# A four-layer graph network: the placing of the edges and the masks of two groups are shared out anew among the engines

## The chip, the cores and the metric

The kernel runs on one core of a Trainium2 chip. The core has a TensorE (PE in the profile, with its weight loads as PEld), a VectorE (DVE), a ScalarE (ACT), a GpSimd (POOL) and a SyncE (SP), which only issues DMAs; ScalarE and GpSimd issue DMAs too (ACTq, POOLq). Each engine runs its own instructions in order and waits for others by semaphores. The metric is the device time of one execution in microseconds, the median over several.

## The reference, cut to what matters

A graph of 3125 nodes with 128 features and 100,000 edges, sorted by their destination, goes through four layers; each takes the layer norm and relu of x and adds its output to x.

```python
edge_index = jnp.stack([src, dst])
h = jnp.maximum(_layernorm(x, axis=-1), 0.0)
x = x + _L0_gnn_ref(h, edge_index, ...)                  # two attention layers of 4 heads
h = jnp.maximum(_layernorm(x, axis=-1), 0.0)
x = x + _L1_gnn_ref(h, edge_weight, weights, src, dst)   # three steps of a recurrence with the weighted adjacency
h = jnp.maximum(_layernorm(x, axis=-1), 0.0)
x = x + _L2_gnn_ref(h, src, dst, ...)                    # three rounds of mean over neighbours
h = jnp.maximum(_layernorm(x, axis=-1), 0.0)
x = x + _L3_gnn_ref(h, edge_index, edge_type_16, ...)    # a message of each edge, relu, mean by destination
```

One attention layer of `_L0_gnn_ref`, with a loop edge at each node:

```python
e = jax.nn.leaky_relu(al_src[src] + al_dst[dst], NEG_SLOPE)
m = jax.ops.segment_max(e, dst, num_segments=N)
w = jnp.exp(e - m[dst])
denom = jax.ops.segment_sum(w, dst, num_segments=N)
out = jax.ops.segment_sum(h[src] * (w / denom[dst])[:, :, None], dst, num_segments=N)
```

## The kernel before, in words

**Blocks and slots.** Nodes are cut into 25 blocks of 128. The adjacency is handled as 25 x 25 pairs of a destination block `db` and a source block `sb`. Each pair has `CAP[db]` slots of 128 lanes in a table in HBM (`self.table`, one row of 64 bytes for each lane). An edge's place is (base of its pair, in slots) times 128, plus its rank within the pair: the rank's upper part chooses the slot, its lower seven bits the lane.

**Placing the edges** (`place_edges`, from line 936). The edge arrays are loaded as 112 rows of 896 (line 955 the body, 956 the last row), after GpSimd has filled the ends of the tiles (953). dst, edge_weight and the shifted dst go by SP's queue, src and edge_type by ScalarE's. The load of x (`load_x`, lines 113 to 115, called in `graph_and_layer0`) is in SP's queue as well, and a fill of the table with -1 (`table<-none`, line 961, 10.9 MB). VectorE then takes blocks and parities out of the indices (968 to 981), counts how runs go on from row to row (989 to 998), and works in two halves of columns (`HALVES`: 512 and 384 of the 896): for each half the **block terms** `cap` and `base` as sums of steps over db (1037 to 1048), the ranks by 13 rounds of a masked running sum (1053 to 1056), the place out of rank, cap and base (1060 to 1081), then a transpose and the integer indices (1087, 1088). GpSimd **scatters** the edges by 782 indirect DMAs of 128 rows (1096), in the order `ORDER`: destination blocks from 5 up first, blocks 0 to 4 last. Each block needs a run of these scatters, `LOW[db]` to `ENDS[db]`. A **test** on VectorE (1107 to 1118) counts the edges below each block and notes in `self.bad` if those runs wouldn't do; if anything in `bad` is set at the end, a general version of the kernel runs.

**Building and attending** (`graph_and_layer0`). After the layer norm and the first projection (lines 1425, 1426 and on), the groups of destination blocks (5 to 8), (9 to 12), ... (21 to 24), (0 to 2), (3, 4) are taken in turn. `build_block` loads a block's slots (1167, one buffer), transposes the keys (1173), makes one-hot matrices on VectorE (1190, 1192) and multiplies them on TensorE (1204, 1207) into counts and weights, which ScalarE takes out (1211, 1212). For blocks below 6, ScalarE also copies rows (1177) and lanes (`wide_dl`, 1181). A **count check** on ScalarE (1217) sees whether any count is above 15. `attend` makes, for each head and each source block, a mask of the group's destinations and multiplies it on TensorE (1379). In the first attention VectorE makes each mask (1365, reading `ps_row` in PSUM and the counts). In the second attention, after all building, two of three masks are VectorE's and every third is ScalarE's and GpSimd's: sign and relu (1359, 1360), then the product with the counts (1362); ScalarE needs a copy of the row in SBUF for it (1483).

**Order.** The order of the instructions on each engine is not that of the code alone: the framework places an instruction whose operands are free where its engine has room (in the profile the fill of `rank`, line 1050, and of `beyond`, line 1113, stand at 1.1 and 1.95 us, ahead of the loads).

Layer 1 (from line 1488) streams the weights back from HBM, layer 2 (1622) multiplies by the counts in SBUF (1722) for groups of five blocks, layer 3 (1821) fetches messages.

Of the kernel before, what the change touches and what calls it, by code (L numbers as in the profile page):

```python
# [18 lines left out]
P = 128  # L19
# [21 lines left out]
GB = 5  # L41
# [23 lines left out]
BATCH = 8  # L65
SL, DL, WT, TYPE = 0, 1, 2, 5
# [834 lines left out]
class FastGnn(Gnn):  # L901
# [24 lines left out]
    def place_edges(self, placed):  # L926
# [9 lines left out]
        with ExitStack() as s:  # L936
# [20 lines left out]
            nc.gpsimd.memset(rec, 0.0)  # L957
# [40 lines left out]
            V.tensor_copy(carry, ps[:A, :n_pair])  # L998
# [14 lines left out]
            nc.scalar.copy(sb, sb_i)  # L1013
            d0, d1 = tile("d0"), tile("d1")
# [15 lines left out]
            t_cap, t_base, t_step, t_rank, t_r, t_hi, t_lane, t_level = (tile(m, dt) for m, dt in names)  # L1030
            idx = {}
            for i, (q0, n0) in enumerate(HALVES):
                lo, hi = q0 * P, (q0 + n0) * P
                cut = lambda t: t[:, lo:hi]

                cap, base, step, of_db = cut(t_cap), cut(t_base), cut(t_step), cut(db)
                V.tensor_scalar(cap, of_db, 24.0, 8.0, op0=OP.is_gt, op1=OP.mult)
                V.tensor_scalar(cap, cap, 1.0, None, op0=OP.add)
                V.tensor_scalar(base, of_db, float(N_SLOTS[-1]), None, op0=OP.mult)
                for d in range(NB - 1):  # L1040
                    for _ in range(CAP[d] - CAP[d + 1]):
                        V.scalar_tensor_tensor(cap, of_db, d + 0.5, cap, op0=OP.is_lt, op1=OP.add)
                    more = N_SLOTS[d] - N_SLOTS[d + 1]
                    if more:
# [22 lines left out]
                whole_of(hi_i, r_i, OP.arith_shift_right, 7)  # L1067
                whole_of(r_i, r_i, OP.bitwise_and, 127)
# [35 lines left out]
            left = t_level  # L1104
# [5 lines left out]
            upto = work.tile([P, NB], F32, name="upto")  # L1110
            V.tensor_copy(upto, ps[:, :NB])
            beyond = work.tile([P, 2, NB], F32, name="beyond")
            V.memset(beyond, 0.0)
# [21 lines left out]
    def open_build(self, s, counts):  # L1135
        nc, tc = self.nc, self.tc
        self.counts = counts.tile([P, NB, NP], FP8, name="counts8")
        self.weights = self.dram.tile([NB, P, NP], F32, name="weights")
        self.wide = self.dram.tile([2, sum(N_SLOTS[:WIDE]) * P], BF16, name="wide")
        one = self.b_one = s.enter_context(tc.tile_pool(name="build", bufs=1))  # L1140
        self.b_slots = s.enter_context(tc.tile_pool(name="build_s", bufs=1))
        self.b_hot = s.enter_context(tc.tile_pool(name="build_hot", bufs=2))
        self.b_out = s.enter_context(tc.tile_pool(name="build_out", bufs=3))
        self.b_ps = s.enter_context(tc.tile_pool(name="build_ps", bufs=2, space=PSUM))
        self.b_keys = s.enter_context(tc.tile_pool(name="build_keys", bufs=1, space=PSUM))
        self.lane16 = one.tile([P, P, 2], BF16, name="lane16")
        nc.vector.tensor_copy(self.lane16, bc(self.lane[:, :, None], [P, P, 2]))
        self.minus_most = one.tile([P, 1], F32, name="minus_most")
        nc.vector.memset(self.minus_most, -MOST)
        self.above = one.tile([P, NB], F32, name="above")  # L1150
        self.junk = one.tile([P, NB, P], FP8, name="junk")

    def build_block(self, db):
# [28 lines left out]
        for x0 in range(0, n_slots, BATCH):  # L1182
# [10 lines left out]
            for x in range(k):  # L1193
# [15 lines left out]
                if last and (j == 1 or sb == NB - 1):  # L1209
# [3 lines left out]
                    if sb % 4 == 3 or sb == NB - 1:  # L1213
# [3 lines left out]
        nc.scalar.activation(self.junk, self.counts[:, :, db * P : (db + 1) * P], AF.Relu, bias=self.minus_most,  # L1217
                             accum_out=self.above[:, db : db + 1], saturate=False)
# [115 lines left out]
    def attend(self, suffix, a, b, pools):  # L1334
# [4 lines left out]
        n = b - a  # L1339
        at, cols = slice(a, b), slice(a * P, b * P)  # L1340
# [3 lines left out]
        for q in range(n):  # L1344
            wide = u_tile()
            for sb in range(NB):
                nc.tensor.matmul(wide[:, : HEADS * 3 * F1], lhsT=self.counts[:, sb, (a + q) * P : (a + q + 1) * P],  # L1347
                                 rhs=parts[:, sb, :, :, F1:], start=(sb == 0), stop=(sb == NB - 1))
            V.tensor_reduce(u[:, q], wide[:, : HEADS * 3 * F1].rearrange("p (h s f) -> p h f s", h=HEADS, s=3),
                            axis=AX.X, op=OP.add)  # L1350
        sums = None
        for i in range(HEADS):
            row, own = row_of(lambda j: bc(self.sd[:, a + j, 1, i : i + 1], [P, P]), n)

            def mask(sb, row=row, own=own, i=i):

                if beside and sb % 3 == 2:
                    above = beside[0].tile([P, most * P], BF16, name="above0")[:, : n * P]
                    nc.scalar.activation(above, own, AF.Sign, bias=self.sd[:, sb, 0, i : i + 1])
                    nc.scalar.activation(above, above, AF.Relu)  # L1360
                    over = beside[1].tile([P, most * P], BF16, name="over")
                    nc.gpsimd.tensor_tensor(over[:, : n * P], above, self.counts[:, sb, cols], op=OP.mult)  # L1362
# [45 lines left out]
    def graph_and_layer0(self, counts, node):  # L1408
# [3 lines left out]
        with ExitStack() as s:  # L1412
            one = s.enter_context(tc.tile_pool(name="l0", bufs=1))
            self.open_attention(one)
            with ExitStack() as s2:
# [3 lines left out]
                super().load_x()  # L1419
# [10 lines left out]
            with ExitStack() as s2:  # L1430
# [196 lines left out]
    def layer2(self):  # L1627
        nc, tc = self.nc, self.tc
        last = 3 * D
        with ExitStack() as s:  # L1630
# [79 lines left out]
            for g in range(GN):  # L1710
# [3 lines left out]
                prepare(g, 0)  # L1714
            for i in range(3):
                n = last + (i == 0)
                ready = []
                for g in range(GN):
                    for db in range(g * GB, (g + 1) * GB):
# [10 lines left out]
                        nc.vector.scalar_tensor_tensor(own[:, db, :], t, inv, own[:, db, :], op0=OP.mult, op1=OP.add)  # L1730
                    finish(g, i)
# [3 lines left out]
                if i == 1:  # L1735
                    self.message_weights(one, ps_msg)
# [298 lines left out]
```

## Time and profile before

| what | us |
|---|---|
| median of 3 runs | 3201.25 (3200.83 to 3203.47) |
| the profiled execution | 3195.56 |
| its span, first to last instruction | 3193.8 |
| busy in it: PE, PEld | 2561.2, 1825.5 |
| busy in it: DVE, ACT, POOL | 2296.6, 917.4, 1445.2 |
| scatters (L1096) on POOL, 782 | 773.6 busy, 336.7 idle before them |
| masks on DVE (L1365), 1040 | 699.3 |
| masks' products on POOL (L1362), 160 | 211.3 |

The mean granted clock of TensorE was 0.959. By stage: edges and placing to about 175 us, first projection to 233, building and the first attention to about 1305, the second attention to 1725, layer 1 to 2200, layer 2 to 2640, layer 3 to the end.

How to read the lines: a timeline line has the start and the duration in us, the engine, the line of the code, the operation, output<-inputs, the shape, how many were merged, and in brackets how long the engine was idle before and what ended that. A line of the groups has the count after "x", then the busy time in us and the mean in ns of one, then the idle time before them with its releasers. "PEld" is a weight load, "SPq" an instruction on SP's DMA queue. The slices cut the span into 40 parts of 80 us; a digit is the busy share in tenths.

### The profile page before, as it was taken

What the parts mean: (1) busy time and instruction counts of PE and PEld (TensorE: products, weight loads), DVE (VectorE), ACT (ScalarE), POOL (GpSimd) and SP (SyncE); (2) the same over time, 40 slices, a digit from 0 to 9 for tenths busy, and PEclk for the clock granted to TensorE, in tenths of its full rate; (3) what the DMA queues carried; (4) which work ended last, traced back from release to release, by engine and by line L of the source; (5) the groups of instructions that cost most, each with busy time, mean ns of one, the idle gap of its engine ahead of it and who ended that gap; (6) DMA issues with size and microseconds to landing.
All of it is one profiled execution on the core that took longest, in us unless ns stands there. A gap on an engine that the chain in (4) does not pass through costs nothing. (4 is left out here: it accounts for less than half of the span.)

```text
span 3193.8 us, 52069 instructions
## 1 busy us (share of the span) xinstructions
PE 2561.2 (80%) x20788; PEld 1825.5 (57%) x20788; DVE 2296.6 (72%) x4015; ACT 917.4 (29%) x1785; POOL 1445.2 (45%) x1394
## 2 busy tenths in 40 slices
PE   0018787878787788798886999997999976989898
PEld 0017464646455655477675444445555546888897
DVE  7979999999989899899997010405455575666766
ACT  3035050505140212476665000002120212333333
POOL 1577777777777700055553000000120106777775
PEclk9979999999999999899999999998999997999999
DMA  6013130303131101000002878781000004444443
GB/s 187 14 18 98 25 98 20 98 20 101 31 94 28 51 32 62 1 2 1 1 1 80 298 272 302 273 301 45 1 1 1 5 18 138 130 139 133 128 131 85
DMA packets 127742, 276.54 MB, mean 87 GB/s; under 512 B 28645, under 2 KB 68468, under 8 KB 116532
## 3 DMA queue, kind: packets, MB, share of 16 engines
q1 hardware_dynamic: 62982, 198.30, 18.9%
q0 software_dynamic: 37856, 32.76, 4.8%
q10 hardware_dynamic: 26652, 42.05, 3.7%
q8 instruction: 165, 2.70, 0.4%
q14 instruction: 87, 0.71, 0.1%
HBM read 210.00 MB, written 63.02 MB: 85 GB/s over the span
## 5 line engine op out<-in xcount | busy, mean ns | idle before, releaser
L1096 POOL DMA_INDIRECT table<-rec,idx x782 | 773.6, 989 | 336.7 <-issue 237.4
L1365 DVE SCALAR_TENSOR_TENSOR over<-ps_row,minus,counts 128x512 bf16<-128x512 f32 (+3 forms) x1040 | 699.3, 748 | 15.9 <-ACT row L1483 12.0
L1379 PE MATMUL ps_acc<-parts,over 128*128 128x198 bf16 x5000 | 571.4, 251 | 134.1 <-POOL over L1362 34.7
L1379 PEld LDWEIGHTS <-over 128*128 128x128 bf16 x5000 | 391.8, 98 | 309.7 <-DVE over L1365 231.9
L1910 POOL DMA_INDIRECT m_far<-pre,src x401 | 397.8, 992 | 259.1 <-DVE skips L923 137.2
L1207 PE MATMUL ps_cw<-oh_w,oh_d 128*128 128x128 bf16 x4050 | 385.9, 224 | 56.7 <-DVE oh_w L1192 52.1
L1533 PE MATMUL ps_sum<-g,node 128*128 128x512 f32 (+1 forms) x1050 | 413.2, 552 | 12.9 <-DMA g<-weights 12.9
L1362 POOL TENSOR_TENSOR over<-above,counts 128x640 bf16<-128x640 bf16 x160 | 211.3, 1329 | 392.0 <-ACT above L1360 265.2
L1207 PEld LDWEIGHTS <-oh_d 128*128 128x128 bf16 x4050 | 303.8, 100 | 90.9 <-issue 68.7
L1204 PE MATMUL ps_cw<-oh_d,oh_s 128*128 128x128 bf16 x1350 | 299.0, 224 | 48.2 <-ACT w_out L1212 24.7
L1722 PE MATMUL ps_agg<-l_parts,counts 128*128 128x384 bf16 (+1 forms) x1875 | 317.3, 327 | 14.0 <-POOL l_parts L923 14.0
L1192 DVE TENSOR_TENSOR oh_w<-oh_s,keys 128x1024 bf16<-128x1024 bf16 (+2 forms) x561 | 325.4, 633 | 0.0
L1533 PEld LDWEIGHTS ps_sum<-g,node 128*128 128x128 f32 x1050 | 189.8, 192 | 222.1 <-issue 208.4
L1722 PEld LDWEIGHTS <-counts 128*128 128x128 fp8e4 x1875 | 183.5, 98 | 134.5 <-issue 11.3
L1754 POOL IOTA of_i<- 96x1 int32 x1 | 0.1, 135 | 480.2 <-PE ps_sum L1609 480.2
L1211 ACT ACTIVATE counts<-ps_cw 128x256 fp8e4<-128x256 f32 (+1 forms) x325 | 122.7, 378 | 303.9 <-PE ps_cw L1207 294.4
L1931 PE MATMUL agg_far<-m_far,oh_far 128*128 128x128 f32 x1246 | 173.8, 287 | 11.6 <-ACT m_far L1917 7.1
L1892 PE MATMUL agg_wide<-m_wide,oh_wide 128*128 128x128 f32 x1100 | 160.3, 289 | 26.5 <-ACT m_wide L1889 17.9
L1204 PEld LDWEIGHTS <-oh_s 128*128 128x128 bf16 x1350 | 133.6, 100 | 80.9 <-issue 49.9
L1347 PEld LDWEIGHTS <-counts 128*128 128x128 fp8e4 x1250 | 112.1, 98 | 102.3 <-ACT counts L1211 19.9
L1885 PE MATMUL ps_m<-skips,src_hot 128*128 128x128 bf16 x1650 | 159.3, 224 | 9.1 <-DVE src_hot L1875 9.1
L1931 PEld LDWEIGHTS agg_far<-m_far,oh_far 128*128 128x128 f32 x1246 | 156.6, 199 | 13.6 <-ACT m_far L1917 9.0
(353 smaller groups left out, 3532.1 us busy)
## 6 DMA issues: line engine op xcount, KB each, us to landing
g<-weights SPq DMA_DIRECT2D x75, 1024.0 KB
g<-weights SPq DMA_DIRECT2D x75, 576.0 KB
weights<-w_out ACTq DMA_DIRECT2D x150, 256.0 KB
src_row<-wide SPq DMA_DIRECT2D x32, 512.0 KB
table<-rec,idx POOLq DMA_INDIRECT x782
type_row<-wide SPq DMA_DIRECT2D x32, 384.0 KB
table<-none SPq DMA_DIRECT2D x1, 10864.0 KB
type_row<-types SPq DMA_DIRECT2D x25, 384.0 KB
```

What stands on the lines that cost most here:

```text
L1096: st = nc.gpsimd.indirect_dma_start(out=self.table, out_offset=bass.IndirectOffsetOnAxis(ap=idx[k][:, p : p + 1], axis=0), in_=rec[:, (k * ...
L1192: nc.vector.tensor_tensor(oh_w[:, t, :h], oh_s[:, :h], key(WT + t), op=OP.mult)
L1204: nc.tensor.matmul(ps[:, 0, j, :], lhsT=oh_s[of], rhs=oh_d[of], start=(j == c == 0), stop=last, skip_group_check=True)
L1207: nc.tensor.matmul(ps[:, 1, j, :], lhsT=oh_d[of], rhs=oh_w[:, t][of], start=False, stop=(last and t == 2), skip_group_check=True)
L1362: nc.gpsimd.tensor_tensor(over[:, : n * P], above, self.counts[:, sb, cols], op=OP.mult)
L1365: V.scalar_tensor_tensor(over[:, : n * P], row, minus[:, sb, i : i + 1], self.counts[:, sb, cols], op0=OP.is_gt, op1=OP.mult)
L1379: nc.tensor.matmul(banks[j // 2][:, j % 2, : 3 * F2], lhsT=over[:, j * P : (j + 1) * P], rhs=parts[:, sb, i].rearrange("p s f -> p (s f)") ...
L1533: nc.tensor.matmul(ps[:, c0 // 512, :m], lhsT=node[:, b, :], rhs=g[:, c0 - lo : c0 - lo + m], start=(b == 0), stop=(b == NB - 1))
L1722: nc.tensor.matmul(ps[:, :n], lhsT=self.counts[:, sb, db * P : (db + 1) * P], rhs=parts[:, sb, :n], start=(sb == 0), stop=(sb == NB - 1))
L1892: nc.tensor.matmul(agg, lhsT=oh[:, j, :], rhs=m[:, j, :], start=(x == 0), stop=(x == n_slots - 1))
L1910: nc.gpsimd.indirect_dma_start(out=m[:, j, :], out_offset=None, in_=pre, in_offset=bass.IndirectOffsetOnAxis(ap=src_of[:, a + j : a + j + ...
L1931: nc.tensor.matmul(agg[d], lhsT=oh[:, c - lo, :], rhs=m[:, c - a, :], start=(c == LOW[d]), stop=(c == ENDS[d] - 1))
```

## The change

It has these parts:

- The loads of x wait until `carry` is made (`self.begun`); the fill of `rec` comes after that of `none`.
- The block terms of both halves are made by GpSimd, from operations with two constants and additions, ahead of the scatters.
- The test is made by ScalarE: the sum of the sign of (2d + 1 - 2 db) for each d, against limits in that measure; 50 small fills make the limits.
- The rank within a slot is no longer the lane: lane = (53 * rank + 5 * sb) mod 128, one more VectorE instruction for each half, and one on ScalarE for 5 * sb.
- In the last two groups of the first attention, blocks 0 to 2 and 3 and 4, every third mask is made by ScalarE and GpSimd as in the second attention, with a copy of the row in SBUF.
- The count check moves from the build to layer 2, one after each of 25 blocks' sums in groups 1 to 3.

```diff
...
-            nc.gpsimd.memset(rec, 0.0)
             per = BASE[NB] // P
             none = work.tile([P, 14 * ROOM], BF16, name="none")
             nc.gpsimd.memset(none, -1.0)
+            nc.gpsimd.memset(rec, 0.0)
...
-            V.tensor_copy(carry, ps[:A, :n_pair])
+            self.begun = V.tensor_copy(carry, ps[:A, :n_pair]).ins
...
+            first = tile("first")
+            nc.scalar.activation(first, sb_i, AF.Copy, scale=5.0)
...
+            G = nc.gpsimd
+            for q0, n0 in HALVES:
+                cut = lambda t: t[:, q0 * P : (q0 + n0) * P]
+                cap, base, step, of_db = cut(t_cap), cut(t_base), cut(t_step), cut(db)
+                G.tensor_scalar(base, of_db, float(N_SLOTS[-1]), None, op0=OP.mult)
+                G.tensor_scalar(cap, of_db, 24.0, 8.0, op0=OP.is_gt, op1=OP.mult)
+                for d in range(NB - 1):
+                    more = N_SLOTS[d] - N_SLOTS[d + 1]
+                    if more:
+                        G.tensor_scalar(step, of_db, d + 1.0, float(more), op0=OP.min, op1=OP.mult)
+                        G.tensor_tensor(base, base, step, op=OP.add)
+                    if CAP[d] > CAP[d + 1]:
+                        G.tensor_scalar(step, of_db, d + 0.5, float(CAP[d] - CAP[d + 1]), op0=OP.is_lt, op1=OP.mult)
+                        G.tensor_tensor(cap, cap, step, op=OP.add)
+                G.tensor_scalar(cap, cap, 1.0, None, op0=OP.add)
+                G.tensor_tensor(step, cut(sb), cap, op=OP.mult)
+                G.tensor_tensor(base, base, step, op=OP.add)
...
-                V.tensor_scalar(cap, of_db, 24.0, 8.0, op0=OP.is_gt, op1=OP.mult)
-                V.tensor_scalar(cap, cap, 1.0, None, op0=OP.add)
-                V.tensor_scalar(base, of_db, float(N_SLOTS[-1]), None, op0=OP.mult)
-                for d in range(NB - 1):
-                    for _ in range(CAP[d] - CAP[d + 1]):
-                        V.scalar_tensor_tensor(cap, of_db, d + 0.5, cap, op0=OP.is_lt, op1=OP.add)
...
-                        V.tensor_scalar(step, of_db, d + 1.0, float(more), op0=OP.min, op1=OP.mult)
-                        V.tensor_add(base, base, step)
-                V.tensor_tensor(step, cut(sb), cap, op=OP.mult)
-                V.tensor_add(base, base, step)
...
+                V.scalar_tensor_tensor(r_i, r, float(TURN), cut(first), op0=OP.mult, op1=OP.add)
                 whole_of(r_i, r_i, OP.bitwise_and, 127)
...
+            odd = work.tile([P, NB], F32, name="odd")
+            nc.gpsimd.iota(odd, pattern=[[2, NB]], base=1, channel_multiplier=0, allow_small_or_imprecise_dtypes=True)
...
-                V.tensor_scalar(left, db, d + 0.5, None, op0=OP.is_lt, op1=OP.add, accum_out=sums[:, d : d + 1])
+                nc.scalar.activation(t_level, db, AF.Sign, bias=odd[:A, d : d + 1], scale=-2.0, accum_out=sums[:, d : d + 1])
...
-            for d in range(NB):
-                V.tensor_scalar(beyond[:, 0, d : d + 1], upto[:, d : d + 1], float(ENDS[d] * P), None, op0=OP.is_gt)
-                if d:
-                    V.tensor_scalar(beyond[:, 1, d : d + 1], upto[:, d - 1 : d], float(LOW[d] * P), None, op0=OP.is_lt)
+            V.tensor_tensor(beyond[:, 0], ps[:, :NB], limit[:, 0], op=OP.is_gt)
+            V.tensor_tensor(beyond[:, 1], ps[:, :NB], limit[:, 1], op=OP.is_lt)
...
-        nc.scalar.activation(self.junk, self.counts[:, :, db * P : (db + 1) * P], AF.Relu, bias=self.minus_most,
-                             accum_out=self.above[:, db : db + 1], saturate=False)
...
-                super().load_x()
+                nc.vector.memset(self.x[:, NB - 1, :], 0.0)
+                x = self.a["x"]
+                for ld in (nc.sync.dma_start(self.x[:, : NB - 1, :], x[: (NB - 1) * P, :].rearrange("(b p) f -> p b f", p=P)),
+                           nc.sync.dma_start(self.x[:TAIL, NB - 1, :], x[(NB - 1) * P :, :])):
+                    self.wait_for(ld.ins, self.begun)
...
+                    rows = s3.enter_context(tc.tile_pool(name="gat_d", bufs=1))
+                    beside = [s3.enter_context(tc.tile_pool(name=f"gat_b{n}", bufs=n)) for n in (2, 3)]
...
+                    def two_rows(term, n):
+                        own = rows.tile([P, 3 * P], F32, name="row")[:, : n * P]
+                        whole, _ = row_of(term, n)
+                        nc.scalar.copy(own, whole)
+                        return whole, own
...
+                    shared = pools[:4] + (two_rows, 4, beside)
...
-                        self.attend(1, a, b, pools)
-                    nc.vector.tensor_reduce(self.bad[:, 1:2], self.above, axis=AX.X, op=OP.add)
+                        self.attend(1, a, b, shared if b <= FIRST else pools)
...
+                        if unseen and 0 < g < GN - 1:
+                            b = unseen.pop()
+                            nc.scalar.activation(junk, self.counts[:, :, b * P : (b + 1) * P], AF.Relu, bias=minus_most,
+                                                 accum_out=above[:, b : b + 1], saturate=False)
...
```

More of the change, by code (lines that the diff above doesn't have):

```diff
@@ L65 @@
 BATCH = 8
+TURN = 53
 SL, DL, WT, TYPE = 0, 1, 2, 5
@@ L1034, in place_edges @@
                 cut = lambda t: t[:, lo:hi]
-                cap, base, step, of_db = cut(t_cap), cut(t_base), cut(t_step), cut(db)
-                V.tensor_scalar(cap, of_db, 24.0, 8.0, op0=OP.is_gt, op1=OP.mult)
-                V.tensor_scalar(cap, cap, 1.0, None, op0=OP.add)
-                V.tensor_scalar(base, of_db, float(N_SLOTS[-1]), None, op0=OP.mult)
-                for d in range(NB - 1):
-                    for _ in range(CAP[d] - CAP[d + 1]):
-                        V.scalar_tensor_tensor(cap, of_db, d + 0.5, cap, op0=OP.is_lt, op1=OP.add)
-                    more = N_SLOTS[d] - N_SLOTS[d + 1]
-                    if more:
-                        V.tensor_scalar(step, of_db, d + 1.0, float(more), op0=OP.min, op1=OP.mult)
-                        V.tensor_add(base, base, step)
-                V.tensor_tensor(step, cut(sb), cap, op=OP.mult)
-                V.tensor_add(base, base, step)
+                cap, base = cut(t_cap), cut(t_base)
                 rank = cut(t_rank)
@@ L1101, in place_edges @@
                 self.placed[c] = st.ins
-            left = t_level
+            odd = work.tile([P, NB], F32, name="odd")
+            nc.gpsimd.iota(odd, pattern=[[2, NB]], base=1, channel_multiplier=0, allow_small_or_imprecise_dtypes=True)
+            limit = work.tile([P, 2, NB], F32, name="limit")
+            V.memset(limit[:, 1], -float(A * EC))
+            for d in range(NB):
+                V.memset(limit[:, 0, d : d + 1], float(2 * ENDS[d] * P - A * EC))
+                if d:
+                    V.memset(limit[:, 1, d - 1 : d], float(2 * LOW[d] * P - A * EC))
             sums = work.tile([A, NB], F32, name="sums")
             for d in range(NB):
-                V.tensor_scalar(left, db, d + 0.5, None, op0=OP.is_lt, op1=OP.add, accum_out=sums[:, d : d + 1])
+                nc.scalar.activation(t_level, db, AF.Sign, bias=odd[:A, d : d + 1], scale=-2.0, accum_out=sums[:, d : d + 1])
             ps = psum.tile([P, P], F32, name="ps_small")
             nc.tensor.matmul(ps[:, :NB], lhsT=self.ones[:A], rhs=sums, start=True, stop=True)
-            upto = work.tile([P, NB], F32, name="upto")
-            V.tensor_copy(upto, ps[:, :NB])
             beyond = work.tile([P, 2, NB], F32, name="beyond")
-            V.memset(beyond, 0.0)
-            for d in range(NB):
-                V.tensor_scalar(beyond[:, 0, d : d + 1], upto[:, d : d + 1], float(ENDS[d] * P), None, op0=OP.is_gt)
-                if d:
-                    V.tensor_scalar(beyond[:, 1, d : d + 1], upto[:, d - 1 : d], float(LOW[d] * P), None, op0=OP.is_lt)
+            V.tensor_tensor(beyond[:, 0], ps[:, :NB], limit[:, 0], op=OP.is_gt)
+            V.tensor_tensor(beyond[:, 1], ps[:, :NB], limit[:, 1], op=OP.is_lt)
             V.tensor_reduce(self.bad[:, :1], beyond.rearrange("p i d -> p (i d)"), axis=AX.X, op=OP.add)
@@ L1147, in open_build @@
         nc.vector.tensor_copy(self.lane16, bc(self.lane[:, :, None], [P, P, 2]))
[L1148 to L1151, printed above, removed]
     def build_block(self, db):
@@ L1339, in attend @@
         n = b - a
+        wide = GW if most == GB else 3 * P
         at, cols = slice(a, b), slice(a * P, b * P)
@@ L1344, in attend @@
         for q in range(n):
-            wide = u_tile()
+            ps = u_tile()
             for sb in range(NB):
-                nc.tensor.matmul(wide[:, : HEADS * 3 * F1], lhsT=self.counts[:, sb, (a + q) * P : (a + q + 1) * P],
+                nc.tensor.matmul(ps[:, : HEADS * 3 * F1], lhsT=self.counts[:, sb, (a + q) * P : (a + q + 1) * P],
                                  rhs=parts[:, sb, :, :, F1:], start=(sb == 0), stop=(sb == NB - 1))
-            V.tensor_reduce(u[:, q], wide[:, : HEADS * 3 * F1].rearrange("p (h s f) -> p h f s", h=HEADS, s=3),
+            V.tensor_reduce(u[:, q], ps[:, : HEADS * 3 * F1].rearrange("p (h s f) -> p h f s", h=HEADS, s=3),
                             axis=AX.X, op=OP.add)
@@ L1357, in mask @@
                 if beside and sb % 3 == 2:
-                    above = beside[0].tile([P, most * P], BF16, name="above0")[:, : n * P]
+                    above = beside[0].tile([P, wide], BF16, name="above0")[:, : n * P]
                     nc.scalar.activation(above, own, AF.Sign, bias=self.sd[:, sb, 0, i : i + 1])
                     nc.scalar.activation(above, above, AF.Relu)
-                    over = beside[1].tile([P, most * P], BF16, name="over")
+                    over = beside[1].tile([P, wide], BF16, name="over")
                     nc.gpsimd.tensor_tensor(over[:, : n * P], above, self.counts[:, sb, cols], op=OP.mult)
@@ L1714, in layer2 @@
                 prepare(g, 0)
+            minus_most = one.tile([P, 1], F32, name="minus_most")
+            nc.vector.memset(minus_most, -MOST)
+            above = one.tile([P, NB], F32, name="above")
+            junk = one.tile([P, NB, P], FP8, name="junk")
+            unseen = list(range(NB))
             for i in range(3):
@@ L1735, in layer2 @@
                 if i == 1:
+                    nc.vector.tensor_reduce(self.bad[:, 1:2], above, axis=AX.X, op=OP.add)
                     self.message_weights(one, ps_msg)
```

## The prediction

> **What bounds the kernel now.** I read the 40 slices first, then the groups, then the timeline of VectorE, GpSimd and the SP queue up to 1345 us. The slices say which engine is full in which stage:
>
> ```profile
> DVE  7979999999989899899997010405455575666766
> POOL 1577777777777700055553000000120106777775
> ```
>
> A slice is 80 us. VectorE is at 9 tenths from the first slices to about 1730 us, the end of layer 0, so up to there a microsecond counts if VectorE or what it waits for gets shorter. GpSimd is at 7 tenths from slice 3 to slice 14: these are the 782 scatters. From 1730 us on TensorE is the full engine, and there only the moved count check is touched.
>
> The timeline shows the start of the chain:
>
> ```profile
> 2.11 6.70 DVE L92 TENSOR_SCALAR ident<-jp 128x128 f32<-128x128 int32 x1
> 2.98 5.33 POOL L957 MEMSET rec<- 128x6296 bf16 x1
> 13.17 3.35 SPq L955 DMA_DIRECT2D raw_dst<-in_dst_dram  x1
> 28.48 0.63 DVE L968 TENSOR_SCALAR db_i<-raw_dst 112x896 int32<-112x896 int32 x1 [18.75 <-DMA raw_dst<-in_dst_dram]
> 108.30 1.26 POOL L1096 DMA_INDIRECT table<-rec,idx  x1 [98.65 <-DVE cap L1042]
> ```
>
> Edges land at 28.48, after the load of x; VectorE then works 79.8 us without a gap until the first scatter at 108.30. The build begins at 233.13 (first slots load). Whether the build hangs on VectorE or on the scatters is read from the slots loads of blocks 8 and 9, each of which needs a run of scatters:
>
> ```profile
> 289.00 0.97 POOL L1096 DMA_INDIRECT table<-rec,idx  x1 [0.30 <-issue]
> 291.43 0.27 SPq L1167 DMA_DIRECT2D slots<-table  x1
> 301.11 0.51 PE L1173 MATMUL keys<-ident,slots 50*128 50x50 bf16 x5
> 322.11 0.97 POOL L1096 DMA_INDIRECT table<-rec,idx  x1 [0.30 <-issue]
> 324.42 0.27 SPq L1167 DMA_DIRECT2D slots<-table  x1
> 328.71 0.48 PE L1173 MATMUL keys<-ident,slots 50*128 50x50 bf16 x5 [0.47 <-DMA slots<-table]
> ```
>
> 289.00 is the 133rd scatter, the last that block 8 needs by its LOW and ENDS; the load goes 1.4 us after its end. Slots take 4.7 us to be usable (233.13 to TensorE's 237.84), so block 8 has 301.11 - 291.43 - 4.7 = 5.0 us of slack. The 159th scatter (322.11) releases block 9, and there TensorE already waits. So at this place VectorE can come at most some 2 to 5 us further ahead of the scatters, and **the start of the scatters, not the work of VectorE, limits what the front can gain**. Later the slack is wide: block 10 loads at 356.25 and is transposed at 419.28; block 0's last scatter (885.22) is 34 us before TensorE takes its slots (921.19).
>
> **The front, part by part.** *Edges first.* The x load leaves the head of SP's queue, so the edge loads can go after their fills, at about 2 us instead of 13.17. A 400 KB slots load takes 4.7 us; five edge loads share the engines, 2 MB at the 279 GB/s of the window 20 to 50 us is 7 us, so edges land at 7 to 10 us. VectorE can't start before 8.84 to 9.7, because the clearing of rec holds its first operation (the 6.70 us above, against 0.89 for the next); that stays, as the clearing only changes place with a 0.46 us one. I take 10 (9.5 to 13, with 50 new small memsets of 0.06 us that should fall into the idle time before). Gain 18.5. What x now waits for is hidden: its first reader is at 174.97, and the fill of the table that it now queues behind ends around 66 (35.35 + 30.76, the issue of types) less the 18 us. Behind x in SP's queue stand types, the two orders (read in layer 3 alone) and weights used at 180.
>
> *Block terms leave VectorE.* Half 0 has 20 operations, 11.87 us of durations, 10.4 by start-to-start; of half 1, eleven stand before the first scatter, 4.4 us. Added: one multiply-add for the lanes, 0.6 (nearest row L1053, 0.68). Chain from edges to scatter: 79.8 - 10.4 - 4.4 + 0.6 = 65.6 us.
>
> *Block terms on GpSimd.* 42 instructions, 20 of two tensors, 22 of one tensor with two constants. Two-tensor price: L921 on POOL takes 1.35 us for 640 elements, 2.11 ns each: 10 x (512 + 384) x 2.11 = 18.9 us. The one-tensor form is in no row. From below: the clearing of rec, 5.33 us for 6296, 0.85 ns; from above the two-tensor 2.11. It reads one stream where these read none and two, so I take the middle, 1.5: 11 x 896 x 1.5 = 14.8 (8.4 to 20.8). Sum 33.7 (27.3 to 39.7). If this ran beside VectorE it would cost nothing, being done about 40 us after the edges. But these rows of layer 2 show that it doesn't:
>
> ```profile
> 2369.23 1.53 POOL L1704 TENSOR_TENSOR skips<-skips,l_own 128x640 f32<-128x640 f32 x1 [0.76 <-DVE l_own L1700]
> 2369.40 2.04 DVE L1702 TENSOR_TENSOR l_h<-l_own,skips 128x640 f32<-128x640 f32 x1
> 2370.72 1.93 POOL L921 TENSOR_TENSOR rest<-z,l_parts 128x640 f32<-128x640 f32 x1
> ```
>
> L1702 has two tensors in SBUF and takes 0.82 us when GpSimd is idle; here it ends 0.68 us after GpSimd's, so it was held for 1.22 of GpSimd's 1.53; then GpSimd's next one is held in turn (1.93 for 1.35). They alternate. The masks L1365, with one operand in PSUM, run at 0.83 us beside L1362 unharmed. In the chain after the edges nearly all of VectorE's work is of the first sort (L989, L1053, the scan L1055, L1056: two SBUF tensors). So I let each of the 42 hold VectorE for its time less 0.15: 33.7 - 6.3 = **27.4 us** (21.0 to 33.4; with no hold at all, 0).
>
> The Trainium skill, "SBUF — State Buffer", section "Who interferes with whom", says the same against this edit: a VectorE instruction with two SBUF inputs and a GpSimd instruction that reads SBUF exclude each other for the whole instruction. By it the sum has the 27.4; by the thought that engines run side by side, 0. The trace shows the hold for tensor_tensor and scalar_tensor_tensor; for the scan no row shows it.
>
> *First scatter:* 10 + 65.6 + 27.4 = 103.0 against 108.30: **5.3 us earlier** (from 11.7 earlier to 3.7 later). VectorE's 20 operations were cheaper than GpSimd's 21 that now stand in their way.
>
> *The test on ScalarE.* It takes 25 x (1.085 + 0.08), some 28 us, and 49 small compares, 3 us, off VectorE. On ScalarE 25 signs of 896: L1359 takes 0.824 for 640, so 1.03 plus part of the 0.19 of the accumulator read, some 28 us. They write level_f, so they follow its last read in half 1, about 31 us after the first scatter: 134 to 162. Queued behind them are the squares of the layer norm, before at 177.69; they would come 15 us earlier and the build up to 19 earlier. That is more than the scatters allow, so it hides: VectorE waits for slots instead. *Lead:* build at block 9 follows the scatters with 2.5 us more lead than now (0 to 5). **Front: 5.3 + 2.5 = 7.8.**
>
> *Scrambled lanes* change addresses alone. A scatter goes each 1.27 us, 0.97 and 0.30 of issue, whether or not VectorE is busy in the build; between 940 and 970 us its queue uses 4.3% of the DMA engines. Landing would have to become over 20 times dearer to count. Zero.
>
> **The end of layer 0.** *Masks.* 8 of 25 masks of 8 heads leave VectorE. Rows, by start-to-start: 9.55 us for 18 masks of 128x384, 0.53; 9.09 for 23 of 128x256, 0.39. 32 x 0.53 + 32 x 0.39 = 29.5 us. VectorE is without gaps there (1150 to 1195: 45 of 45 us). The new chain per mask, scaled from
>
> ```profile
> L1359 ACT ACTIVATE above<-row,sd 128x640 bf16<-128x640 f32 x160 | 131.4, 824 | 40.9 <-POOL over L1362 39.1
> L1360 ACT ACTIVATE above<-above 128x640 bf16<-128x640 bf16 x160 | 114.2, 731 | 3.3
> ```
>
> with the fixed 0.16 us of ScalarE's copies: sign and relu 1.06 us at 384 and 0.82 at 256, product 0.80 and 0.53. Per head at 256 ScalarE has 8 x 0.82 + 0.37 = 6.9 us, VectorE 17 x 0.39 + 0.56 = 7.2: ScalarE is nearly as full as VectorE, and it waits in its queue for slots (5.86 and 2.86 us at 1121 and 1153). So I take three quarters, **22** (12 to 29). GpSimd's scatters are over at 1119, the masks start at 1146: 27 us of cover.
>
> *Count check.* In the build L1217 stands ahead of the copy of wide_dl, for which VectorE waits:
>
> ```profile
> 1069.51 2.97 ACT L1217 ACTIVATE junk<-counts,minus_most 128x3200 fp8e4<-128x3200 fp8e4 x1
> 1072.73 0.69 DVE L1190 TENSOR_TENSOR oh_s<-lane,keys 128x1024 bf16<-128x1024 bf16 x1 [2.26 <-ACT wide_dl L1181]
> ```
>
> Three such waits, 2.26 + 2.24 + 1.88, of which 0.4 each stays: **5** (2 to 6). In layer 2 it is 25 x 3.1 us on ScalarE, beside 4.1 us of TensorE for each block; it can delay a square, and what reads that has a whole group (20 us) of cover. Cost 2 (0 to 6); without the cover it would be up to 3 us for each of the five groups.
>
> **Sum:** -7.8 - 22 - 5 + 2 = -33. The profiled execution took 3195.56 us (span 3193.8 and 1.8 around it), which becomes 3163; the median of the runs is 5.7 above it, so 3201.25 - 33 = **3168**. Its own range, all terms at their ends: 3150 to 3190.
>
> **Rivals.** *No hold:* GpSimd's terms run beside VectorE. The masks L1365 show that some pairs do; the rows of 2369 speak against it for this pair. First scatter at 75.6, 32.7 earlier: 3201 - 35 - 22 - 5 + 2 = 3141. *Masks bring nothing,* because ScalarE and GpSimd deliver late and TensorE waits for each third mask, as it does for 34.7 us of L1379's idle time in layer 0's second half: 3190. *The edges don't come sooner* (the loads stay behind something else, edges at 28): first scatter at 121, front +10: 3186. *GpSimd's block terms are slow,* the one on the other side: a comparison with two constants is in no row of POOL. At 6 ns an element the 42 take 78 us, first scatter at 147, and blocks 5 to 9 follow it: +39 - 2.5 - 25 = 3213. It decides slower from about 5.5 ns on. For it: no row prices it, L1704 takes 2.05 where L921 takes 1.35. Against it: every POOL row of data lies between 0.85 and 2.2 ns, L1704's excess is the hold.
>
> **How the numbers follow.** Chances: forecast 0.50, no hold 0.17, masks nothing 0.12, edges not sooner 0.08, GpSimd slow 0.13. The range takes in all but the slow case and half a tail of the no-hold case: 3138 to 3203. A measurement of this kernel tells about 0.2%, 6.4 us, from no change. Faster: nearly all of the forecast, the no-hold case and most of the two in between, 0.75; slower 0.15; same 0.10.
>
> **What would show it.** Edges' first operation at 10 us (step one). POOL's instructions of the block terms alternating with L989 and L1053, which grow from 1.09 and 0.68 us (the hold); if these keep their times, the no-hold case. First scatter at 97 to 112. Slots loads of blocks 8 and 9 directly after their scatters, VectorE waiting for keys there. From the first mask of blocks 0 to 2 to the end of blocks 3 and 4's, before 1146.2 to 1305, some 24 us less. The forecast is wrong if the first scatter is before 90 or after 120, or if the last two groups take as long as before.

## The result and the profile after

The changed kernel takes 3214.12 us (median of 6 runs, 3208.61 to 3219.95), the kernel before 3201.02 in the same comparison (6 runs): a ratio of 1.0037, 95% interval 1.0026 to 1.0048. It became slower by some 13 us, where 3168 was forecast. The profiled execution has a span of 3210.2 us against 3193.8, 16.4 more; its granted clock is 0.953 against 0.959.

First the 40 slices of the kernel after, now of 80.3 us each:

```profile
DVE  9768999999989898899994010414455574666766
ACT  4343030304121155766662000007420222223333
POOL 8677777777777632355551000001120106777775
```

Two things are new. GpSimd is busy in the first slice already (its block terms), and ScalarE has a 7 in the slice from 2167 us on, where layer 2 begins. To find the 16 us, the span is cut at instructions that stand in both kernels: the first load of weights in layer 1 is issued when layer 0 is done, the load of `upd_b` waits for the end of layer 1, and `pre<-z` for the sums of layer 2. The timeline of SP's queue before, then after:

```profile
1733.53 1.30 SPq L1531 DMA_DIRECT2D g<-weights  x3
...
2203.44 0.33 SPq L448 DMA_DIRECT2D w_L_gnn_upd_b<-in_L_gnn_upd_b_dram  x1
...
2546.23 48.44 SPq L1805 DMA_DIRECT2D pre<-z  x3
```

```profile
1710.42 1.29 SPq L1553 DMA_DIRECT2D g<-weights  x3
...
2181.26 0.33 SPq L449 DMA_DIRECT2D w_L_gnn_upd_b<-in_L_gnn_upd_b_dram  x1
...
2555.63 24.42 SPq L1838 DMA_DIRECT2D pre<-z  x2
```

| stage | before | after | difference |
|---|---|---|---|
| to the end of layer 0 | 1733.5 | 1710.4 | -23.1 |
| layer 1 | 469.9 | 470.8 | +0.9 |
| layer 2 | 342.8 | 374.4 | **+31.6** |
| layer 3 | 647.6 | 654.6 | +7.0 |

Layer 0 gains 23 us; layer 2 loses 32, and only the count check was put there. The timeline of ScalarE at the head of layer 2, after (L1761 is the check, L1240 a square of the layer norm, L1681 and L1689 the copies between TensorE's transposes and products of the first projection):

```profile
2183.59 2.96 ACT L1761 ACTIVATE junk<-counts,minus_most 128x3200 fp8e4<-128x3200 fp8e4 x1 [21.88 <-DVE mean L1237]
2186.45 0.19 ACT L1761 ACTIVATION_READ_ACCUMULATOR junk<-counts,minus_most 128x1 f32 x1
2186.55 1.35 ACT L1240 ACTIVATE square<-l_h 128x640 f32<-128x640 f32 x2
2187.80 2.95 ACT L1761 ACTIVATE junk<-counts,minus_most 128x3200 fp8e4<-128x3200 fp8e4 x1
...
2195.14 0.75 ACT L1681 COPY yT<-ps_t 128x512 f32<-128x512 f32 x2
...
2196.71 2.95 ACT L1761 ACTIVATE junk<-counts,minus_most 128x3200 fp8e4<-128x3200 fp8e4 x1
...
2199.66 0.35 ACT L1689 COPY z<-ps_w 128x256 f32<-128x256 f32 x1
```

In the code a check stands behind each of 15 blocks' sums in the first round and of 10 in the second. On the engine all 25 stand at the head, 2183.59 to 2279.77, most of them one to four rows of short instructions apart: the counts had been ready since layer 0, and the constant `minus_most`, in a tile of layer 2, was written at 2183.3. None of them reads anything that layer 2 computes. The rows of the stretch of 100 us from the start of layer 2 say what this does. The columns are: stretch, its length, then for PE, PEld, DVE, ACT and POOL the busy time and the number of instructions, PE's clock, DMA share and GB/s. Before, then after, and after up to the place where TensorE has come as far as before:

```profile
2203.40:2303.40 100.00, 82.63 (x447) 53.53 (x448) 58.02 (x149) 25.92 (x64) 17.07 (x13) 0.93 0.07 20
```

```profile
2181.30:2281.30 100.00, 56.68 (x253) 38.78 (x254) 35.91 (x104) 94.91 (x112) 13.75 (x11) 0.83 0.07 20
2181.30:2313.00 131.70, 88.38 (x445) 57.51 (x446) 58.48 (x158) 96.80 (x116) 15.93 (x12) 0.87 0.06 15
```

ScalarE went from 26 to 95 of 100 us, and TensorE, which is the full engine of this layer, from 83 to 57. The 447 instructions that TensorE got through in 100 us before take 132 after, so the 32 us are lost here, at the head. TensorE was idle for 43 us of them instead of 17, and busy for 88.4 us instead of 82.6, at a granted clock of 0.87 instead of 0.93.

Now the front. The timeline after, several engines together:

```profile
12.26 0.63 DVE L969 TENSOR_SCALAR db_i<-raw_dst 112x896 int32<-112x896 int32 x1 [2.56 <-DMA raw_dst<-in_dst_dram]
16.76 0.63 DVE L969 TENSOR_SCALAR sb_i<-raw_src 112x896 int32<-112x896 int32 x1 [3.87 <-DMA raw_src<-in_src_dram]
...
66.26 1.26 POOL L1049 TENSOR_TENSOR cap<-cap,step 112x512 f32<-112x512 f32 x1
66.27 2.33 DVE L1064 TENSOR_TENSOR_SCAN run<-same,carry,mask 112x512 f32<-112x512 f32 x1
67.47 1.91 POOL L1046 TENSOR_TENSOR base<-base,step 112x384 f32<-112x384 f32 x1
68.52 1.41 DVE L1062 SCALAR_TENSOR_TENSOR mask<-pair,unit 112x512 f32<-112x512 f32 x1
...
70.88 1.26 DVE L1064 TENSOR_TENSOR_SCAN run<-same,carry,mask 112x512 f32<-112x512 f32 x1
...
112.63 1.98 POOL L1107 DMA_INDIRECT table<-rec,idx  x1 [15.80 <-issue]
...
167.65 0.19 DVE L1129 TENSOR_TENSOR beyond<-ps_small,limit 128x25 f32<-128x25 f32 x1 [29.21 <-PE ps_small L1127]
168.36 1.55 DVE L1236 TENSOR_REDUCE mean<-x 128x5 f32<-128x640 f32 x2 [0.20 <-DVE bad L1131]
...
326.88 0.27 SPq L1176 DMA_DIRECT2D slots<-table  x1
```

Four things are to be seen. The edges land 16 us sooner, but src 4.5 us behind dst. GpSimd and VectorE alternate: the scan takes 2.33 us when it has to wait for GpSimd's addition, 1.26 when it does not. The first scatter is at 112.63, 4.3 later than before, and block 9's slots follow at 326.88, 2.5 later (why less than 4.3, see the last section). And VectorE stands still for 29.21 us until ScalarE's test is through, before it begins the layer norm.

The masks: the first of blocks 0 to 2 and of blocks 3 and 4, after (before they stood at 1146.2 and 1258.4):

```profile
1146.71 2.18 DVE L1373 SCALAR_TENSOR_TENSOR over<-ps_row,minus,counts 128x384 bf16<-128x384 f32 x4
...
1242.88 1.65 DVE L1373 SCALAR_TENSOR_TENSOR over<-ps_row,minus,counts 128x256 bf16<-128x256 f32 x4
```

From the first to the start of layer 1's loads it is 563.7 us after and 587.3 before: 23.6 us less.

### The profile page after: what moved, and what is told of

It reads as the page before. It is cut to its first block, busy times and chain, and to the rows that moved or that the text cites. A ratio compares the mean times of both kernels' runs of the same rounds, so it can differ in the third digit from the quotient of the medians.

```text
span 3210.2 us, 52216 instructions
## 1 busy us (share of the span) xinstructions
PE 2552.9 (80%) x20788; PEld 1842.3 (57%) x20788; DVE 2247.4 (70%) x3864; ACT 1004.7 (31%) x1972; POOL 1568.8 (49%) x1501
## 5 line engine op out<-in xcount | busy, mean ns | idle before, releaser
L1373 DVE SCALAR_TENSOR_TENSOR over<-ps_row,minus,counts 128x512 bf16<-128x512 f32 (+3 forms) x976 | 670.4, 761 | 20.5 <-ACT row L1505 12.0
L1387 PE MATMUL ps_acc<-parts,over 128*128 128x198 bf16 x5000 | 552.5, 252 | 122.8 <-POOL over L1370 34.0
L1387 PEld LDWEIGHTS <-over 128*128 128x128 bf16 x5000 | 400.2, 98 | 268.9 <-DVE over L1373 186.1
L1943 POOL DMA_INDIRECT m_far<-pre,src x401 | 405.2, 1011 | 259.1 <-DVE skips L924 137.2
L1370 POOL TENSOR_TENSOR over<-above,counts 128x640 bf16<-128x640 bf16 (+2 forms) x224 | 260.0, 1169 | 323.3 <-PE ps_acc L1387 159.7
L1367 ACT ACTIVATE above<-row,sd 128x640 bf16<-128x640 f32 (+2 forms) x224 | 166.8, 747 | 59.5 <-POOL over L1370 56.5
```

What stands on the lines that cost most here:

```text
L1387: nc.tensor.matmul(banks[j // 2][:, j % 2, : 3 * F2], lhsT=over[:, j * P : (j + 1) * P], rhs=parts[:, sb, i].rearrange("p s f -> p (s f)") ...
L1943: nc.gpsimd.indirect_dma_start(out=m[:, j, :], out_offset=None, in_=pre, in_offset=bass.IndirectOffsetOnAxis(ap=src_of[:, a + j : a + j + ...
```

## The experiments

"Bound" below means the changed kernel with each check made to wait for its block's sums. The first four kernels ran on a chip on which every kernel, the one before too (4354.93 us), took a third longer; there only ratios and layers 1 and 2 are read, and the end of layer 0 only to compare two kernels of that chip (layers 0 and 3 are much longer there).

### The count check

The check bound to its block's sums (run twice, the second time beside the kernels of the next sections):

```diff
-                        nc.vector.scalar_tensor_tensor(own[:, db, :], t, inv, own[:, db, :], ...)
+                        summed = nc.vector.scalar_tensor_tensor(own[:, db, :], t, inv, own[:, db, :], ...)
...
-                            nc.scalar.activation(junk, ...)
+                            seen = nc.scalar.activation(junk, ...)
+                            self.wait_for(seen.ins, summed.ins)
```

> The changed kernel, each count check made to wait for the sums of its block in layer 2. Theory (the 25 checks, 77 us of ScalarE, stand at the head of layer 2 among the copies that its first projection needs, and cost 32 us there): from the end of layer 1 to the first copy of layer 3 374 becomes 343 us, the whole 3214 becomes 3183 (3179 to 3188). Rival one (a check costs its 3 us wherever it stands in layer 2, for each group of five): 15 us come back, 3198. Rival two (the loss is not the checks): 3210 or more.

> The changed kernel with each count check bound to its block's sums, timed once more, beside the next three. Theory: 32 of the 32 us come back, 3182 (3176 to 3188) where the kernel before has 3201, a ratio of 0.994. Rival (only half comes back): 3198.

And the kernel before with the move of the check alone: L1217 and its tiles out of the build, the changed kernel's lines into layer 2.

> The kernel before with the move of the count check alone. Theory: +32 in layer 2, -2 to -5 in the build: 3201 becomes 3229 (3224 to 3233). Rival (the checks harm only together with the other parts): 3198 to 3206.

Measured, layer 2 from `upd_b` to `pre<-z`: 341.9 us with bound checks (3117.66 to 3459.53) and 374.4 in the kernel before with the move alone (3140.19 to 3514.55), on the same chip. The ratios to the kernel before are 0.9941 (0.9919 to 0.9963) and 1.0086 (1.0055 to 1.0117). The second run of bound checks gives 3173.37 us against 3198.90, ratio 0.9923 (0.9909 to 0.9937), and layer 2 takes 342.1. ScalarE's timeline there, and the row of 100 us from the start of layer 2:

```profile
2190.17 0.75 ACT L1681 COPY yT<-ps_t 128x512 f32<-128x512 f32 x2 [2.31 <-PE ps_t L1680]
...
2252.66 2.96 ACT L1761 ACTIVATE junk<-counts,minus_most 128x3200 fp8e4<-128x3200 fp8e4 x1 [0.24 <-DVE l_own L1758]
...
2259.65 2.96 ACT L1761 ACTIVATE junk<-counts,minus_most 128x3200 fp8e4<-128x3200 fp8e4 x1 [3.94 <-DVE inv_col L1754]
```

```profile
2179.00:2279.00 100.00, 82.03 (x447) 53.04 (x448) 57.97 (x150) 44.09 (x77) 16.52 (x13) 0.93 0.07 20
```

The same 25 checks with the same 2.96 us cost nothing once they stand beside TensorE's sums: TensorE has 82.03 of 100 us again. Both rivals fall: the loss comes back whole, not half, and it appears in the kernel before without any other part. So it is not the work of the check that cost 32 us, but its place in ScalarE's queue. The total came back by more than forecast (3173 for 3182); layers 0, 1 and 3 were 6 us shorter together than in the profile after (-2.7, +0.5 and -4.1), which the check does not explain.

### The masks and the check in the build

The kernel before without the check, and the same with the masks of the last two groups shared (the tiles and `two_rows` as in the change):

> The kernel before without the count check, whose 25 instructions are left out. Theory: only the waits for wide_dl of the last blocks go, 2 to 5 us: 3197. Rival (in blocks 5 to 24, too, the check holds up the build): 10 us or more, 3191 or less. Second rival (hidden anyway): 3201.

> The kernel before with the masks of the last two groups shared, and without the count check (left out). Theory (masks bring 22 to 24): 23 less than the kernel without the check alone, 3174. Rival (the masks' gain seen at the end of layer 0 comes from other parts of the change): within 5 of the kernel without the check, 3192 or more.

> The kernel before with the shared masks and without the count check (left out), once more, beside these. Theory (masks 23, the check's place in the build 2 to 4): 3175 (3171 to 3179). Rival one (the last two groups gain only what the missing waits for wide_dl bring): 3195. Rival two (all of it the masks, the check nothing): 3171 or less.

Without the check alone: ratio 0.9987 (0.9969 to 1.0005), -4 us, with an interval that takes in nothing; the size is not settled. With the masks: 0.9945 (0.9924 to 0.9965), and again on another chip 0.9913 (0.9899 to 0.9926), 3176.55 for 3203.23, where 3175 was expected. On the slow chip layer 0 ends at 2672.80 without and at 2646.10 with the masks, 26.7 earlier (the medians are 19 apart). In the second comparison it ends at 1706.50; in the profile before it was 1733.53, 27.0 later, for masks and missing check together, forecast at 22 + 5. The masks bring about what was forecast, and without any other part.

### Edges first, and the block terms

The kernel before with the edges' loads first (the x loads wait for `carry`, `rec` is cleared after `none`), and the bound kernel with the block terms on VectorE again (the lines of the kernel before, 1037 to 1048):

> The kernel before with the edges' loads first, and nothing else. Theory: edges at 12.3, source at 16.8 instead of 28.5, first scatter 10 to 13 earlier, at 96 to 98; the test still takes 28 us of VectorE, so the build follows the scatters with less lead than in the changed kernel: 5 to 11 less, 3193. Rival (the build hangs on VectorE there): within 3 of the kernel before.

> The kernel with bound checks, and the block terms on VectorE again. Theory (GpSimd's 42 instructions hold VectorE for some 24 us, VectorE's own 20 of half 0 cost 10.4): first scatter at 97 to 103 where the changed kernel has 112.6; block 9's slots 10 to 14 earlier; the whole 8 to 14 less than with the terms on GpSimd, 3171. Rival one (VectorE hides it in the build): first scatter as said, but the whole within 3 of it, 3180. Rival two (no hold; the 112.6 are the late edges): first scatter at 117 to 123, the whole 5 more.

Edges first alone: 3188.22 for 3198.90, ratio 0.9965 (0.9951 to 0.9978); first scatter 96.78, block 9's slots 313.17 instead of 324.42. The 11.5 us of the scatter come through to the end almost whole (10.7). Terms on VectorE: 3161.52, ratio 0.9880 (0.9865 to 0.9896), where the bound kernel has 0.9923. Its timeline:

```profile
67.63 1.26 DVE L1059 TENSOR_TENSOR_SCAN run<-same,carry,mask 112x512 f32<-112x512 f32 x1
68.82 0.66 DVE L1057 SCALAR_TENSOR_TENSOR mask<-pair,unit 112x512 f32<-112x512 f32 x1
69.40 0.71 DVE L1060 COPY_PREDICATED rank<-mask,run 112x512 f32<-112x512 int32 x1
...
97.27 1.27 POOL L1102 DMA_INDIRECT table<-rec,idx  x1 [87.47 <-DVE cap L1046]
...
162.37 0.18 DVE L1124 TENSOR_TENSOR beyond<-ps_small,limit 128x25 f32<-128x25 f32 x1 [29.20 <-PE ps_small L1122]
...
316.51 0.27 SPq L1171 DMA_DIRECT2D slots<-table  x1
...
322.12 2.12 DVE L1368 SCALAR_TENSOR_TENSOR over<-ps_row,minus,counts 128x512 bf16<-128x512 f32 x3 [3.69 <-PE ps_acc L1382]
```

The scans have 1.26 us throughout; the first scatter comes 15.2 us earlier than the 112.46 of the bound kernel, block 9's slots 9.4 (316.51 for 325.88; 10 to 14 were expected), and the whole 12 us by the medians. In the profiled execution, the slowest of its four, layer 0 ends only 7.4 us earlier, so what the 15.2 us are worth at the end is known to some 5 us. The last row is the new limit: VectorE waits 3.69 us, as TensorE has block 9's keys in its queue and waits 4.42 us (to 320.79) for the slots that left at 316.51. The hold is shown, the rivals (hidden in the build, no hold) are not what happened. The Trainium skill, "SBUF — State Buffer", section "Who interferes with whom", says that a VectorE instruction with two SBUF inputs contends with a GpSimd instruction that reads SBUF. The trace of the changed kernel agrees, and shows it for the scan (2.33 us for 1.26) and the predicated copy (1.13 for 0.71) as well. Beside GpSimd's terms three operations with one input (L979, L985 and one of L969) also took 1.03 us for 0.62 to 0.68.

### The lanes

The bound kernel with the rank as the lane again (the line with `TURN` and `first` removed):

> The kernel with bound checks, the lane of a slot the rank again (one VectorE instruction less for each half). Theory (addresses alone): within 3 of the kernel with bound checks, scatters paced as before at 1.27 us. Rival (scrambled lanes land cheaper, the pace in the changed kernel of 1.263 against 1.274 is theirs): 4 to 9 more.

3175.07, ratio 0.9928 (0.9914 to 0.9941) against 0.9923: nothing, as forecast. The scatters' pace did not go back to 1.27 us, as the theory had it: the 20 from the 160th on take 25.24 us, 25.26 in the bound kernel, 25.47 in the kernel before and 25.46 with the terms on VectorE. So the slightly quicker pace goes with the terms on GpSimd and not with the lanes; why is open.

### The test

Three kernels on the base of the one with the block terms on VectorE: the test on VectorE again; the test on ScalarE, but written into a tile that is free early; and that one with half 1's block terms and ranks bound behind half 0's indices.

```diff
-                nc.scalar.activation(t_level, db, AF.Sign, bias=odd[:A, d : d + 1], ...)
+                nc.scalar.activation(d1, db, AF.Sign, bias=odd[:A, d : d + 1], ...)
```

```diff
-                    V.scalar_tensor_tensor(mask, cut(pair), float(b), cut(unit), ...)
+                    late(V.scalar_tensor_tensor(mask, cut(pair), float(b), cut(unit), ...))
...
+            def late(op):
+                if i:
+                    self.wait_for(op.ins, self.first_idx)
```

> The kernel with bound checks and with block terms and test both on VectorE. Theory (in the changed kernel VectorE stands idle for 29 us until ScalarE's test is through, so the test costs the path as much there as on VectorE): layer norm begins within 3 us of the 163.2 of the kernel with the test on ScalarE, the whole 3158 (3154 to 3164), none worse than 3161.5. Rival (the test off VectorE is worth part of its 28 us): 3167 or more.

> Bound checks, block terms on VectorE, and the test on ScalarE written into another tile, so that it need not wait for the last read of level_f. Theory (after the stall is gone the scatters still set the end of blocks 5 to 9): layer norm begins at 134 to 140 instead of 163, block 9's slots at 317 as before, the whole within 4 of 3161.5. Rival (the stall is what costs): 3150 or less.

> As the one before, and the block terms and ranks of half 1 wait until the places of half 0 are made. Theory (half 1's instructions stand among half 0's last and put the first scatter off by 5 to 9 us): first scatter at 88 to 92, block 9's slots 3 to 8 earlier, the whole 3157 (3152 to 3160). Rival (what half 1 does later slows the scatters by as much, 1.85 for 1.27 us): 3161 or more.

Test on VectorE: 3162.76, ratio 0.9880 (0.9865 to 0.9895), the same as with the test on ScalarE; the layer norm begins at 164.71 for 163.15. So the move of the test bought nothing: VectorE waits as long as it had worked. The time is 5 above the expected 3158; the kernel before, too, was 4 us slower in that comparison.

Test early: 3172.87, ratio 0.9907 (0.9891 to 0.9922), by the ratios some 9 us **more**, where at most 4 either way were expected. Its timeline:

```profile
63.91 1.04 ACT L1120 ACTIVATE d<-db,odd 112x896 f32<-112x896 f32 x1
...
64.95 0.17 ACT L1062 COPY carry<-run 112x1 f32<-112x1 f32 x1
...
65.15 1.28 DVE L1059 TENSOR_TENSOR_SCAN run<-same,carry,mask 112x512 f32<-112x512 f32 x1 [4.20 <-ACT carry L1062]
...
103.11 1.26 POOL L1102 DMA_INDIRECT table<-rec,idx  x1 [93.32 <-DVE cap L1046]
...
147.97 1.55 DVE L1231 TENSOR_REDUCE mean<-x 128x5 f32<-128x640 f32 x2 [8.38 <-DMA dst_of<-in_order]
```

The stall of 29 us is gone and the layer norm begins 15 us sooner, but that brings nothing, for the slots of block 9 now leave at 322.98. What costs is at 65.15: ScalarE's copy of one column, 0.17 us long, comes behind tests of 1.04 us, and the scan that reads it waits 4.20 us (and 1.00 at the next). The first scatter is 5.8 us later. It is the fault of layer 2 once more: a long piece of filler (work that nobody waits for soon) ahead of a short copy.

Half 1 later: 3174.14, ratio 0.9915 (0.9901 to 0.9928). The first scatter was at 101.18, 1.9 earlier than without the binding, not the 5 to 9 that were expected; the theory was wrong in size. Block 9's slots leave at 317.89, 5 earlier, but the first slots load at 231.33 is 7 later than without the binding, and the whole gains nothing. The traces show where the 5 us go. Without the binding VectorE waits 4.5 us for TensorE and block 9's slots; with it that wait is gone, but the build starts 7 us later, and VectorE has the same 172 us of work up to the load of block 11's slots, which leave at 418.16 instead of 418.48. Some nine more scatters stand ahead of the first load (92 for 83); which of them it waits for stays open. The time is in the rival's range, but not by its cause: 12 scatters took 1.54 us with the binding and 12 without.

**The version that beats both** is the changed kernel with bound checks and the block terms on VectorE: 3161.52 us for 3198.90 (ratio 0.9880, with the test on either engine).

## Why the prediction was wrong

| step | forecast | measured |
|---|---|---|
| edges | at 10 | dst 12.26, src 16.76 |
| hold of VectorE by the block terms | 27.4 | 23 |
| first scatter | 103.0 | 112.63 |
| test on ScalarE | hidden, layer norm 15 earlier | 29.21 idle, 6.6 earlier |
| front, at block 9's slots | -7.8 | +2.5 |
| lanes | 0 | 0 |
| masks | -22 | -23.6 |
| check, in the build | -5 | -4 (-13 to +2, at 4355) |
| check, in layer 2 | +2 (0 to 6) | **+31.6** |

**The step that failed** is the count check in layer 2: "25 x 3.1 us on ScalarE, beside 4.1 us of TensorE for each block", covered by a group of 20 us. The price of one was right (2.96 and 0.19); the place was not. The checks were costed where the code writes them. They read nothing that layer 2 computes, so the framework, which puts an instruction with free operands where its engine has room, put all of them ahead of the sums beside which they are written, into the projection, some 50 us (2203 to 2255 before) in which ScalarE's copies stand between TensorE's transposes and products. The fallback, "up to 3 us for each of the five groups", made the same assumption. With this term at 32 for 2, and all else as forecast, the sum is 3198, just below no change. Of the 46 us between 3168 and 3214 the check is 30, the front 10 and layer 3 is 7; the masks gave 1.6 back.

**The front** is the second term that was mis-sized. Of the 9.6 us between 103.0 and 112.63, 2.3 are the later dst, 3.9 the wait for src (its load goes by ScalarE's queue, and all five were taken to land at 10), and some 7.2 (start to start, from 94.70 to 111.12) are rank rounds of half 1 that stand between half 0's last instructions: the forecast had struck half 1's block terms from there, 4.4 us, and put nothing in their place. The hold, 4.4 smaller, takes part of that back. The hold was right in kind and near in size: in the changed kernel 13 of L990 take 0.35 us more each than the same lines before, 13 of L1062 0.51, 13 scans 0.49, 13 predicated copies 0.29, and three single ones 1.7 together: 23.0 (without the three one-input operations, 1.2 more). The reading that "the start of the scatters, not the work of VectorE, limits what the front can gain" held: a scatter earlier by 11.5 or 15.2 us gave 10.7 and 12, one later by 5.8 cost 9. Half 1 later is the exception: there the build, begun 7 us later, was held by its own work and not by block 9's scatters. So the front ended at +2.5, as the scatters began late. The move of the test says nothing on this reading, for it did not free VectorE: the forecast had queued only ScalarE's squares behind the test, but VectorE's own queue held the layer norm's mean behind L1129, which reads the test's sums (29.21 us). Layer norm came 6.6 us earlier, not 15.

**GpSimd slow**, the rival on the other side, had the right time (3213) for the wrong reason. Its 78 us for the block terms came true, 76.3 from 19.08 to 96.83, a one-tensor form 4.4 to 4.6 ns an element while the two engines alternated, not 1.5. But VectorE first reads a term at 103.62, so the first scatter at 147 did not come about.

**The masks**, the largest term, were right to 2 us (the stretch holds one wait for `wide_dl` in both kernels, 1.88 us before and 1.71 after, so by that wait the missing check has 0.2 of the 23.6), with the rival "masks bring nothing" refuted by two runs. In the build the check's three waits for `wide_dl` became two (6.4 to 3.6 us between 1000 and 1345 us); its whole worth there is not settled.

**Layer 3** was 7.0 longer in the profiled run. Its code is the same in all kernels, and in the nine others that ran at the usual speed it takes between 647.1 and 652.2. So most of the 7.0 lies within what kernels with this same layer differ by; the last 2.4 stay open.

## What to carry to other kernels

Work moved "into the shade" is costed where it will be issued, not where it is written: an instruction that has no open operand is free to be put ahead, and as an engine takes its instructions in order, 3 us of filler ahead of each 0.4 us copy cost 32 us here, and 1 us of filler ahead of a 0.17 us copy 6. Bind it to something late, such as the sums beside which it is to stand. And before work is moved off a full engine, look at what the stage hangs on: here an earlier start of the scatters was worth most of its length, and 28 us taken off VectorE nothing, because VectorE then waited 29 us for the result.

## What the runs showed of the hardware that was not expected

While half 1's ranks are made, scatters and VectorE go in step. A rank round takes VectorE 1.85 us, and beside these rounds 11 scatters of the kernel before (115.51 to 133.98) take 1.54 us and 0.30 of issue each, where a scatter takes 0.97 and 0.30 later. In the changed kernel, where part of half 1's rounds lie ahead of the first scatter, there are 6 such (118.82 to 128.06). The five fewer, 0.57 us each, are worth some 2.9 us, the larger part of why 4.3 us at the first scatter are 1.8 at the 159th (323.86 for 322.11). What ties the two engines is not shown.

On one chip the kernels took 4323 to 4384 us (medians). While the scatters ran, VectorE, ScalarE and TensorE stood still for long stretches, as in this timeline of VectorE in the kernel before without the check ("remote" stands where the profile names no engine that ended the wait):

```profile
568.39 0.69 DVE L1186 TENSOR_TENSOR oh_s<-lane,keys 128x1024 bf16<-128x1024 bf16 x1 [60.98 <-remote]
...
666.38 0.69 DVE L1186 TENSOR_TENSOR oh_s<-lane,keys 128x1024 bf16<-128x1024 bf16 x1 [87.12 <-remote]
```

The scatters nearly kept their pace (1061 ns in the mean, 989 in the kernel before on the usual chip), and the first slots load went at 495.81 instead of 233.13. Layer 3, which has indirect DMAs too, took 847 to 874 us there instead of some 650, while layers 1 and 2 were as long as elsewhere. In none of the ten traces of the usual speed does such a wait appear. What held the engines is not shown by the profile.
